# Layer 1 of a four-layer graph network: another order for the column numbers and the sums

## The chip, the cores and the metric

The kernel runs on one core of a Trainium2 chip. The metric is the device time of one execution in microseconds (us); the median of the runs is given. A core has five engines with a queue each: TensorE (PE in the profile; its weight loads, PEld, overlap with products), VectorE (DVE), ScalarE (ACT), GpSimd (POOL) and SyncE (SP), which here issues transfers. Each engine works through its own queue; engines meet at semaphores.

## The reference

Four layers of a graph network on 2708 nodes with 128 features and one weighted adjacency matrix, `adj`, in which well under one per cent of the entries are not zero. The change concerns layer 1 alone:

```python
def _L1_gnn_ref(node_feats, adj, msg_w, msg_b, upd_w, upd_b, ln_w, ln_b):
    s = node_feats @ msg_w[:, :D].T
    d = node_feats @ msg_w[:, D:].T
    messages = gelu(s[:, None, :] + d[None, :, :] + msg_b)
    aggregated = einsum('ijd,ij->id', messages, adj)
    combined = concatenate([node_feats, aggregated], axis=-1)
    new_feats = combined @ upd_w.T + upd_b
    h = gelu(new_feats) + node_feats
    # ... layer norm of h
# --- layer 1 ---
h = maximum(layernorm(x), 0.0)
x = x + _L1_gnn_ref(h, adj, ...)
```

A message is a gelu of a sum that belongs to a pair of nodes, so it can't be had from one product of matrices; but a message is only needed where `adj` has an entry. Layers 0, 2 and 3 (a plain sum over neighbours, a gated cell, attention) are not touched.

## The kernel before

Layer 0 reads `adj` once and lists, for each row and each block of 124 columns, up to 8 entries (`val`, `col`). Layer 1 works from these lists. Its rows come in 22 tiles of 128 (`NT = 22`) and its columns in 22 blocks (`NB = 22`, `HB = 11`). For each tile and block the entries are packed into up to 128 numbered slots; a 0/1 matrix `sel` says which row a slot belongs to, and a 0/1 matrix `cols` says which column. PE then makes the argument of the gelu of each slot as `sel * s + cols * d` (`s` and `d` split into three bf16 parts, hence three products each), ACT applies the gelu, and PE sums the messages of a row with a matrix `put`, which holds each entry's value in its row.

The steps for a tile, in the order in which they come (cuts are marked):

```python
def rank(t):          # first slot of each row: a product on PE, copies on DVE
    p = rpool.tile([P, CH], F32, tag="r", name="p_r")
    nc.tensor.matmul(p[:, 0:NB], before, rows_n[:, t, :], start=True, stop=True)
    nc.vector.tensor_copy(ends[:, t, :], p[:, 0:NB])
    ...
# describe(t): packs val and col into xb (ACT, DVE "v_r", POOL)
def select_rows(t):   # DVE, then a transfer that shifts sel by one row
    sel = selpool.tile([P, NB, E], BF16, name="sel")
    compare(sel, ends4, ALU.is_ge)
    nc.sync.dma_start(later[0:112, :, :], sel[1:113, :, :])
    ...
def finish_rows(t):   # DVE
    nc.vector.tensor_tensor(sel, sel, later, ALU.subtract)
def fetch(t, half):   # PE brings each slot its row's entries; ACT copies "lead"
    ...
    nc.tensor.matmul(y[:, b, :], st["sel"][:, bb, :], xb[t % 2][:, bb, :], start=True, stop=True)
    ...
def place(t):         # DVE: each slot's column number, value and row
    # ... slot, hot, picked
    nc.vector.tensor_reduce(where, picked[:, :, 3, :], AX.X, ALU.max)
    nc.vector.reduce_sum(value, picked[:, :, 0:3, :], AX.XY)
    mine = once.tile([P, NB, P], BF16, name="mine")
    compare(mine, lead[:, :, 0:R], ALU.is_equal)
def put_values(t):    # POOL: put = mine * value for blocks 0 to 10
    ...
def put_more(t, k):   # ACT: the same for blocks 11 to 21, some in each step
    for b in range(HB + 2 * k, min(HB + 2 * k + 2, NB)):
        nc.scalar.activation(st["put", 1][:, b - HB, :], st["mine"][:, b, :], AF.Identity, scale=st["value"][:, b : b + 1])
def pass_on(t):       # the column numbers are turned on PE and spread to all partitions
    p = rpool.tile([P, 2 * CH], BF16, tag="r", name="p_w")
    nc.tensor.transpose(p[0:NB, 0:E], st.pop("where"), ident_h)
    turned = work.tile([NB, E], BF16, name="where_T")
    nc.scalar.copy(turned, p[0:NB, 0:E])
    passed = wdram.tile([NB, E], BF16, name="passed")
    nc.sync.dma_start(passed, turned)
    st["spread"] = work.tile([P, NB, E], BF16, name="spread")
    nc.sync.dma_start(st["spread"]..., passed....partition_broadcast(P))
def columns(t):       # DVE
    nc.vector.tensor_scalar(st["cols"], st.pop("spread"), part, None, ALU.is_equal)
def sources(k):       # s of two tiles: PE "p_s", DVE "sb" and "s_r", ACT, POOL
    ...
def combine(t, k):    # PE: 4 blocks, each three products with sel and three with cols, into p_m
    ...
def activate(t, k):   # ACT: g = gelu(p_m)
    ...
def gather(t, k):     # PE: agg += g * put, one f32 product for each of 4 blocks (2 in the last
                      # group); the trace counts each f32 product as two
    ...
```

The pool `rpool` has one PSUM buffer, which `p_r`, `p_w`, `p_s` and the updates' `p_u` use in turn. `once` has one buffer per name, `work` two; `g` has three buffers and `p_m` two.

Five tiles are under way at a time. A period combines tile t and prepares those behind it, in six steps (`GB = 6`); the order in the program is the order in each engine's queue:

```python
for k in range(GB):
    if now:
        combine(t, k)
        activate(t, k)
    if k == 0:
        if last:
            gather(t - 1, GB - 1)
            close_tile(t - 1)
        if a:
            rank(t + 3)
    elif now:
        gather(t, k - 1)
    if k in (1, 2) and b:
        fetch(t + 2, k - 1)
    if k == 1 and a:
        describe(t + 3)
    if k == 2:
        if now and t % 2 == 0 and t + 2 < NT:
            sources(t // 2 + 1)
        if a:
            select_rows(t + 3)
        if now and t + 4 < NT:
            count_rows(t + 4)
        updates(t)
    if k == 3 and c:
        columns(t + 1)
    if c:
        put_more(t + 1, k)
    if k == 3 and b:
        place(t + 2)
    if k == 4 and b:
        pass_on(t + 2)
    if k == 4 and a:
        finish_rows(t + 3)
```

Here `now`, `c`, `b` and `a` say that tiles t, t + 1, t + 2 and t + 3 exist, and `last` that t - 1 does. `put_values(t + 1)` stands ahead of the steps. `updates` brings groups of four finished tiles through the layer's update, two small parts per period. Periods -3 to -1 are laid between the steps that end layer 0.

Of the kernel before, what the change touches and what calls it, by code (L numbers as in the profile page):

```python
# [21 lines left out]
BF16 = mybir.dt.bfloat16  # L22
# [8 lines left out]
P = 128  # L31
# [13 lines left out]
NB = (N + JB - 1) // JB  # L45
S = 8
E = P
# [4 lines left out]
def size(t):  # L52
    return min(P, N - t * P)
# [7 lines left out]
def listed_layers(ctx: ExitStack, tc: tile.TileContext, x, adj, w, out, flag):  # L61
# [111 lines left out]
    with tc.tile_pool(name="l0c", bufs=1) as fix:  # L173
# [4 lines left out]
        with (  # L178
# [6 lines left out]
            for gi, (g0, gk) in enumerate(GROUPS):  # L185
# [4 lines left out]
                for q in range(gk):  # L190
                    n = g0 + q
                    m = size(n)
                    a = a4[:, q, :]
# [26 lines left out]
                for j in range(NT):  # L220
                    k = size(j)
# [55 lines left out]
    HB = NB // 2  # L277
    R = 4
    C = 4 * S + R + 1
    with (  # L280
# [55 lines left out]
        def compare(dst, numbers, op):  # L336

            nc.vector.tensor_tensor(  # L338
                dst.rearrange("p b (x r) -> p b x r", r=R),
                count_h.rearrange("p (x r) -> p x r", r=R).unsqueeze(1).to_broadcast([P, NB, P // R, R]),  # L340
                numbers.unsqueeze(2).to_broadcast([P, NB, P // R, R]),
                op,
            )

        def rank(t):
# [3 lines that stand above are left out]
            nc.vector.tensor_copy(ends4, p[:, 0:NB].unsqueeze(2).to_broadcast([P, NB, R]))  # L349
# [35 lines left out]
        def place(t):  # L385

            st = state[t]
            lead = st["lead"]
            slot = work.tile([P, NB], F32, name="slot")
            nc.vector.tensor_scalar(slot, lead[:, :, R], part, -1.0, ALU.subtract, ALU.mult)  # L390
            hot = once.tile([P, NB, S], F32, name="hot")
            nc.vector.tensor_tensor(
                hot,
                count[:, 0:S].unsqueeze(1).to_broadcast([P, NB, S]),
                slot.unsqueeze(2).to_broadcast([P, NB, S]),
                ALU.is_equal,
            )
            picked = once.tile([P, NB, 4, S], F32, name="picked")
            for half, y in enumerate(st.pop("ys")):
                bs = slice(half * HB, (half + 1) * HB)  # L400
                nc.vector.tensor_tensor(
                    picked[:, bs, :, :],
                    y[:, :, 0 : 4 * S].rearrange("p b (q s) -> p b q s", s=S),
                    hot[:, bs, :].unsqueeze(2).to_broadcast([P, HB, 4, S]),
                    ALU.mult,
                )
            value = work.tile([P, NB], F32, name="value")
            where = work.tile([P, NB], BF16, name="where")
            with nc.allow_low_precision("column numbers"):
                nc.vector.tensor_reduce(where, picked[:, :, 3, :], AX.X, ALU.max)  # L410
            nc.vector.reduce_sum(value, picked[:, :, 0:3, :], AX.XY)
            mine = once.tile([P, NB, P], BF16, name="mine")
            compare(mine, lead[:, :, 0:R], ALU.is_equal)
            st["value"], st["where"], st["mine"] = value, where, mine

        def put_values(t):

            st = state[t]
            for half in range(2):
                st["put", half] = putpool.tile([P, HB, P], F32, name="put")  # L420
            nc.gpsimd.tensor_tensor(  # L421
                st["put", 0],
                st["mine"][:, 0:HB, :],
                st["value"][:, 0:HB].unsqueeze(2).to_broadcast([P, HB, P]),
                ALU.mult,
            )

        def put_more(t, k):

            st = state[t]  # L430
            for b in range(HB + 2 * k, min(HB + 2 * k + 2, NB)):
                nc.scalar.activation(  # L432
                    st["put", 1][:, b - HB, :], st["mine"][:, b, :], AF.Identity, scale=st["value"][:, b : b + 1]
                )

        def pass_on(t):

            st = state[t]
# [3 lines that stand above are left out]
            nc.scalar.copy(turned, p[0:NB, 0:E])  # L442
            passed = wdram.tile([NB, E], BF16, name="passed")
            nc.sync.dma_start(passed, turned)
            st["spread"] = work.tile([P, NB, E], BF16, name="spread")
            nc.sync.dma_start(
                st["spread"].rearrange("p b e -> p (b e)"), passed.rearrange("b e -> (b e)").partition_broadcast(P)
            )

        def columns(t):  # L450

            st = state[t]
            st["cols"] = work.tile([P, NB, E], BF16, name="cols")
            nc.vector.tensor_scalar(st["cols"], st.pop("spread"), part, None, ALU.is_equal)
# [35 lines left out]
        def combine(t, k):  # L490

            st = state[t]
            s3 = own_rows[t // 2][0]
            b0 = 4 * k
            n = min(4, NB - b0)
            p = mpool.tile([P, 4, D], F32, name="p_m")
            for b in range(b0, b0 + n):
                kb = width(b)
                for q in range(3):
                    nc.tensor.matmul(  # L500
                        p[:, b - b0, :], st["sel"][:, b, :], s3[:, q, t % 2, :], start=(q == 0), stop=False
                    )
                for q in range(3):
                    nc.tensor.matmul(  # L504
                        p[:, b - b0, :], st["cols"][0:kb, b, :], d3[0:kb, b, q, :], start=False, stop=(q == 2)
                    )
            st["p", k] = p

        def activate(t, k):
            n = min(4, NB - 4 * k)  # L510
            g = three.tile([P, 4, D], F32, name="g1")
            nc.scalar.activation(g[:, 0:n, :], state[t].pop(("p", k))[:, 0:n, :], AF.Gelu)  # L512
            state[t]["g", k] = g

        def gather(t, k):

            st = state[t]
            m = size(t)
            if k == 0 and t % 4 == 0:
                aggs[t // 4] = acc.tile([P, 4, P], F32, name="agg1")  # L520
            agg = aggs[t // 4][:, t % 4, 0:m]
            g = st.pop(("g", k))
            for b in range(4 * k, min(4 * k + 4, NB)):
                put = st["put", b // HB][:, b % HB, 0:m]
                nc.tensor.matmul(agg, g[:, b - 4 * k, :], put, start=(b == 0), stop=False)  # L525
# [62 lines left out]
        def updates(t):  # L588

            for g, (first, k) in enumerate(GROUPS):  # L590
                step = t - (first + k + 1)
                if 0 <= step < STEPS:
                    update(g, step)

        GB = (NB + 3) // 4

        def period(t):

            now, c, b, a = (0 <= t + q < NT for q in range(4))
            last = 0 <= t - 1 < NT  # L600
            if c:
                put_values(t + 1)
            for k in range(GB):
                if now:
                    combine(t, k)
                    activate(t, k)
                if k == 0:
                    if last:
                        gather(t - 1, GB - 1)
                        close_tile(t - 1)  # L610
                    if a:
                        rank(t + 3)
                elif now:
                    gather(t, k - 1)
                if k in (1, 2) and b:
                    fetch(t + 2, k - 1)
                if k == 1 and a:
# [6 lines that stand above are left out]
                    if now and t + 4 < NT:  # L624
                        count_rows(t + 4)
                    updates(t)
                if k == 3 and c:
                    columns(t + 1)
                if c:
                    put_more(t + 1, k)  # L630
                if k == 3 and b:
                    place(t + 2)
                if k == 4 and b:
                    pass_on(t + 2)
                if k == 4 and a:
                    finish_rows(t + 3)

# [262 lines left out]
    with (  # L900
# [135 lines left out]
        last = RUNS[0]  # L1036
# [12 lines left out]
    with tc.tile_pool(name="l3w", bufs=5) as wpool, tc.manual_schedule():  # L1049
        for run, numbers in zip(RUNS[1:], ((2, 3, 4, 5, 0, 1), (2, 3, 4, 5, 0, 1), (2, 3))):  # L1050
# [5 lines left out]
            last = run  # L1056
# [466 lines left out]
```

## Time and profile before

| | us |
|---|---|
| time, median of 3 runs (1163.88 to 1165.95) | 1165.69 |
| span of the profiled execution | 1161.2 |
| PE busy in it | 981.1 |
| DVE busy | 848.1 |
| ACT busy | 487.0 |
| POOL busy | 333.8 |

PE has products in 84% of the span, but the layers have different limits, so layer 1 has to be looked at by itself: its periods lie between 311 and 696 us. L500 and L504 are the products of `combine`, L525 those of `gather`, L440 the turn of the column numbers, L347 and L468 the products of `rank` and `sources`. On DVE, L338 is `compare` (for `sel` and for `mine`), L369 `finish_rows`, L454 `columns`, L410 and L411 `where` and `value`. On ACT, L512 is the gelu and L432 `put_more`; on POOL, L421 is `put_values`. In a line of waits, `A <- B: us, times, longest` means that A stood still until B was done. Columns of a timeline are start, length in us, engine, line, operation, output and inputs, shapes, count, and in brackets the idle time before it with what ended it.

### The profile page before, as it was taken

The numbers are of one execution on the slowest core, as the hardware profiler recorded it, in microseconds if no ns is written. First come the engines' busy times: TensorE is split into PE (matmuls) and PEld (weight loads), VectorE is DVE, ScalarE is ACT, GpSimd is POOL, SyncE is SP. The second block draws the span as 40 slices with busy tenths as digits, with TensorE's granted clock in tenths as the row PEclk, the third lists the DMA queues.
The fourth block names the chain that finished last, engine by engine and source line by source line (L and its number), as shares of the span: only waits on it lengthen the run. The fifth ranks groups of instructions, "written<-read, shape, count | busy, mean of one in ns | idle before, by whom it ended". The sixth has DMA issues, their size and how long they took to land. (4 is left out here: it accounts for less than half of the span.)

```text
span 1161.2 us, 21750 instructions
## 1 busy us (share of the span) xinstructions
PE 981.1 (84%) x7968; PEld 778.4 (67%) x7968; DVE 848.1 (73%) x2948; ACT 487.0 (42%) x1253; POOL 333.8 (29%) x312
## 2 busy tenths in 40 slices
PE   4987987803599998978889897999988999999993
PEld 1554544503488888978789893444457999999872
DVE  5999999988466656676666836565557887897683
ACT  4855656604455555546455452243333110140142
POOL 3111112013324433535334226343331020150042
PEclk9999889655599999989899897999999999999996
DMA  9587787411123222222212106554520000000000
GB/s 363 192 287 266 284 292 249 165 54 55 46 76 101 101 77 79 74 95 82 76 61 92 51 28 236 192 185 164 181 56 1 1 8 1 1 15 6 1 14 13
DMA packets 55297, 125.38 MB, mean 108 GB/s; under 512 B 7414, under 2 KB 19782, under 8 KB 52472
## 3 DMA queue, kind: packets, MB, share of 16 engines
q1 hardware_dynamic: 48590, 121.12, 30.0%
q10 hardware_dynamic: 6590, 2.77, 1.0%
q8 instruction: 64, 1.05, 0.4%
q14 instruction: 53, 0.43, 0.1%
HBM read 77.30 MB, written 30.84 MB: 93 GB/s over the span
## 5 line engine op out<-in xcount | busy, mean ns | idle before, releaser
L804 PE MATMUL att<-hv,wt 128*128 128x129 f32 (+2 forms) x1936 | 242.4, 282 | 9.2 <-DVE wt L772 9.2
L804 PEld LDWEIGHTS att<-hv,wt 128*128 128x128 f32 (+2 forms) x1936 | 223.4, 191 | 26.3 <-DVE wt L772 8.9
L772 DVE SCALAR_TENSOR_TENSOR wt<-row,lift,mask 128x1024 f32<-128x1024 f32 (+5 forms) x176 | 160.0, 939 | 34.0 <-PE att L804 34.0
L500 PE MATMUL p_m<-s,sel 128*128 128x128 bf16 x1452 | 168.4, 226 | 3.0 <-ACT s L323 1.9
L504 PE MATMUL p_m<-d,cols 124*128 124x128 bf16 (+1 forms) x1452 | 168.4, 226 | 0.0
L525 PE MATMUL agg<-put,g 128*128 128x128 f32 (+1 forms) x968 | 144.3, 293 | 10.9 <-ACT g L512 10.9
L196 PE MATMUL acc<-a,hs 128*128 128x512 f32 (+2 forms) x264 | 123.9, 606 | 25.8 <-DMA a<-in_adj 19.0
L525 PEld LDWEIGHTS agg<-put,g 128*128 128x128 f32 x968 | 126.0, 202 | 12.6 <-ACT g L512 12.6
L119 POOL TENSOR_TENSOR n_r<-n_r,minus_half 128x4 f32<-128x4 f32 (+1 forms) x36 | 48.2, 1340 | 295.5 <-DVE n_r L118 281.4
L217 DVE FIND_INDEX8 col<-val,a 128x8 uint16<-128x124 f32 (+1 forms) x441 | 119.9, 286 | 0.0
L512 ACT ACTIVATE g<-p_m 128x512 f32<-128x512 f32 x132 | 73.2, 555 | 110.1 <-PE p_m L504 109.2
L421 POOL TENSOR_TENSOR put<-mine,value 128x1408 f32<-128x1408 bf16 x22 | 79.8, 3629 | 132.7 <-DVE mine L338 125.6
L925 PE MATMUL p_agg<-a,hs 128*128 128x512 f32 (+2 forms) x264 | 110.4, 560 | 7.7 <-DVE n1u_st L116 4.4
L500 PEld LDWEIGHTS <-sel 128*128 128x128 bf16 x1452 | 107.9, 101 | 7.7 <-issue 3.6
L504 PEld LDWEIGHTS <-cols 124*128 124x128 bf16 (+1 forms) x1452 | 107.8, 101 | 0.6 <-issue 0.6
L216 DVE MAX8 val<-a 128x8 f32<-128x124 f32 (+1 forms) x441 | 103.7, 277 | 0.0
L196 PEld LDWEIGHTS acc<-a,hs 128*128 128x128 f32 (+1 forms) x264 | 50.2, 210 | 72.0 <-issue 43.9
L225 PEld LDWEIGHTS p_T<-ident,a 128*128 128x128 f32 x484 | 58.5, 145 | 53.6 <-ACT aT L229 25.6
L225 PE MATMUL p_T<-ident,a 128*128 128x128 f32 x484 | 77.2, 292 | 19.2 <-DMA a<-in_adj 10.0
L229 ACT ACTIVATE aT<-p_T 128x512 f32<-128x512 f32 (+2 forms) x132 | 71.0, 541 | 44.0 <-issue 19.6
L925 PEld LDWEIGHTS p_agg<-a,hs 128*128 128x128 f32 (+1 forms) x264 | 48.3, 195 | 56.0 <-issue 55.0
L432 ACT ACTIVATE put<-mine,value 128x128 f32<-128x128 bf16 x242 | 83.6, 391 | 0.0
(228 smaller groups left out, 1415.7 us busy)
## 6 DMA issues: line engine op xcount, KB each, us to landing
a<-in_adj SPq DMA_DIRECT2D x21, 1354.0 KB
adjT<-aT SPq DMA_DIRECT2D x105, 256.0 KB
a<-adjT SPq DMA_DIRECT2D x20, 1280.0 KB
spread<-passed SPq DMA_DIRECT2D x22, 704.0 KB
later<-sel SPq DMA_DIRECT2D x22, 616.0 KB
later<-sel SPq DMA_DIRECT2D x22, 82.5 KB
adjT<-aT SPq DMA_DIRECT2D x21, 74.0 KB
a<-adjT SPq DMA_DIRECT2D x4, 370.0 KB
```

The costliest lines, as they stand in the source:

```text
L196: nc.tensor.matmul(accs[ci][:, 0:cw], h[0:m, n, :], a[0:m, c : c + cw], start=(n == 0), stop=(n == NT - 1))
L216: nc.vector.max(val[:, n, b, :], ab)
L217: nc.vector.max_index(col[:, n, b, :], val[:, n, b, :], ab)
L225: nc.tensor.transpose(p[0:k, q * P : q * P + m], a4[0:m, q, j * P : j * P + k], ident[0:m, 0:m])
L421: nc.gpsimd.tensor_tensor(st["put", 0], st["mine"][:, 0:HB, :], st["value"][:, 0:HB].unsqueeze(2).to_broadcast([P, HB, P]), ALU.mult,)
L432: nc.scalar.activation(st["put", 1][:, b - HB, :], st["mine"][:, b, :], AF.Identity, scale=st["value"][:, b : b + 1])
L500: nc.tensor.matmul(p[:, b - b0, :], st["sel"][:, b, :], s3[:, q, t % 2, :], start=(q == 0), stop=False)
L504: nc.tensor.matmul(p[:, b - b0, :], st["cols"][0:kb, b, :], d3[0:kb, b, q, :], start=False, stop=(q == 2))
L525: nc.tensor.matmul(agg, g[:, b - 4 * k, :], put, start=(b == 0), stop=False)
L772: nc.vector.scalar_tensor_tensor(wt[0:kj, :], row[0:kj, k, c : c + n], lift[0:kj, j, k : k + 1], mask[0:kj, j, c : c + n], op0=ALU.max, op ...
L804: nc.tensor.matmul(banks[s // 3][0:m, s % 3, :], wt[0:kj, q * P : q * P + m], hv[0:kj, j, k, :], start=(v < 2 and s // 3 not in touched), ...
L925: nc.tensor.matmul(pa[:, 0:n], h[0:k, j, :], a[0:k, j - j0, 0:n], start=(j == 0), stop=(j == NT - 1))
```

## The change

Three things. The turn of the column numbers (`pass_on`) goes from step 4 of the period in which they are found to step 0 of the next one, so that PE need not wait for them; `columns` moves with it, from step 3 (ahead of `place`) to step 4 (behind it). The sums (`gather`) come two groups behind the messages instead of one, so that the gelu has more time; the last two groups of a tile are summed in the next period. And `mine` gets two buffers, so that it can be written while `put_more` still reads the last one, while `spread` needs only one. `put_more` does its eleven blocks in steps 1 to 5 (2, 2, 2, 2, 3) instead of 0 to 5.

```diff
--- before.py
+++ after.py
@@ -409,7 +409,7 @@
             with nc.allow_low_precision("column numbers"):
                 nc.vector.tensor_reduce(where, picked[:, :, 3, :], AX.X, ALU.max)
             nc.vector.reduce_sum(value, picked[:, :, 0:3, :], AX.XY)
-            mine = once.tile([P, NB, P], BF16, name="mine")
+            mine = work.tile([P, NB, P], BF16, name="mine")
             compare(mine, lead[:, :, 0:R], ALU.is_equal)
             st["value"], st["where"], st["mine"] = value, where, mine
 
@@ -428,7 +428,7 @@
         def put_more(t, k):
 
             st = state[t]
-            for b in range(HB + 2 * k, min(HB + 2 * k + 2, NB)):
+            for b in range(HB + (NB - HB) * (k - 1) // (GB - 1), HB + (NB - HB) * k // (GB - 1)):
                 nc.scalar.activation(
                     st["put", 1][:, b - HB, :], st["mine"][:, b, :], AF.Identity, scale=st["value"][:, b : b + 1]
                 )
@@ -442,7 +442,7 @@
             nc.scalar.copy(turned, p[0:NB, 0:E])
             passed = wdram.tile([NB, E], BF16, name="passed")
             nc.sync.dma_start(passed, turned)
-            st["spread"] = work.tile([P, NB, E], BF16, name="spread")
+            st["spread"] = once.tile([P, NB, E], BF16, name="spread")
             nc.sync.dma_start(
                 st["spread"].rearrange("p b e -> p (b e)"), passed.rearrange("b e -> (b e)").partition_broadcast(P)
             )
@@ -604,14 +604,17 @@
                 if now:
                     combine(t, k)
                     activate(t, k)
-                if k == 0:
+                if k < 2:
                     if last:
-                        gather(t - 1, GB - 1)
+                        gather(t - 1, GB - 2 + k)
+                    if k == 0 and c:
+                        pass_on(t + 1)
+                    if k == 0 and a:
+                        rank(t + 3)
+                    if k == 1 and last:
                         close_tile(t - 1)
-                    if a:
-                        rank(t + 3)
                 elif now:
-                    gather(t, k - 1)
+                    gather(t, k - 2)
                 if k in (1, 2) and b:
                     fetch(t + 2, k - 1)
                 if k == 1 and a:
@@ -624,14 +627,12 @@
                     if now and t + 4 < NT:
                         count_rows(t + 4)
                     updates(t)
-                if k == 3 and c:
-                    columns(t + 1)
-                if c:
+                if k > 0 and c:
                     put_more(t + 1, k)
                 if k == 3 and b:
                     place(t + 2)
-                if k == 4 and b:
-                    pass_on(t + 2)
+                if k == 4 and c:
+                    columns(t + 1)
                 if k == 4 and a:
                     finish_rows(t + 3)
```

## The prediction

> **What bounds the kernel now.** I read the table of stretches first, to find the stage the change touches. Layer 1's periods run from 311 to 696 us. Columns: stretch, length, busy time of PE, PEld, DVE, ACT, POOL with counts, granted clock, DMA share, GB/s.
>
> ```profile
> 311.00:696.00 385.00, 343.60 (x4520) 331.70 (x4518) 239.43 (x453) 199.72 (x558) 145.14 (x106) 0.93 0.22 75
> ```
>
> TensorE (PE) is busy 89% of the stage at a mean clock of 0.93: about 41 us idle, and a further loss because part of the work ran slower. VectorE (DVE) is at 62%, so no second engine is full on average. The waits between 320 and 680 us say who stops whom (us in total, times, longest):
>
> ```profile
> ACT g L512 <- PE p_m L504: 100.0, 85, 3.8
> ...
> DVE mine L338 <- ACT put L432: 32.8, 20, 2.3
> ...
> PE p_w L440 <- DVE where L410: 27.5, 16, 3.6
> ...
> PE agg L525 <- ACT g L512: 10.9, 10, 2.1
> ```
>
> PE has two waits only: turning the column numbers waits for `where` (27.5 us, in 16 of 20 periods), and the sums wait for the gelu before them (10.9 us). The change aims at both, and its second `mine` buffer at the 32.8 us of DVE. What such a wait does next is in PE's timeline (start, us, engine, line, operands, count, idle before):
>
> ```profile
> 457.60 1.16 PE L525 MATMUL agg<-put,g 128*128 128x128 f32 x8 [0.57 <-ACT g L512]
> 461.21 0.28 PE L440 MATMUL p_w<-ident_h,where 128*22 128x128 bf16 x1 [2.45 <-DVE where L410]
> 461.43 0.50 PE L500 MATMUL p_m<-s,sel 128*128 128x128 bf16 x3
> ...
> 467.83 0.33 PE L500 MATMUL p_m<-s,sel 128*128 128x128 bf16 x3
> ```
>
> After the 2.45 us wait three products take 0.50 to 0.53 us instead of 0.33, until 467.83: starts of three-product groups are 0.32 us apart instead of 0.17, so half speed. Over the stage such stretches add up to 34.5 us, about 17 us lost.
>
> DVE's timeline of the same period shows why `where` is late:
>
> ```profile
> 453.42 0.69 DVE L475 TENSOR_TENSOR sb<-p_s,msg_b 128x512 f32<-128x512 f32 x1 [2.56 <-PE p_s L468]
> ...
> 458.33 0.95 DVE L454 TENSOR_SCALAR cols<-spread,part 128x2816 bf16<-128x2816 bf16 x1
> 459.19 0.23 DVE L390 TENSOR_SCALAR slot<-lead,part 128x22 f32<-128x22 bf16 x1
> ...
> 460.82 0.34 DVE L410 TENSOR_REDUCE where<-picked 128x22 bf16<-128x176 f32 x1
> 461.08 0.69 DVE L411 TENSOR_REDUCE value<-picked 128x22 f32<-128x528 f32 x1
> 463.70 1.63 DVE L338 TENSOR_TENSOR mine<-count_h,lead 128x2816 bf16<-128x2816 bf16 x1 [1.93 <-ACT put L432]
> ```
>
> DVE idles 2.56 us for PE's products `p_s` of step 2 and then works without a break to `where`. So the period is a loop of two legs: PE from the turn at 443.22 to `sb` at 453.42 (10.20 us), DVE from `sb` to the end of `where` at 461.16 (7.74), a hand-over of 0.05; the sum is the 17.99 us between turns. In periods without source rows the DVE leg starts at `v_r` instead, which waits for ScalarE (ACT) and so for PE's step 1.
>
> **What the Trainium skill says.** "TensorE: Matmul & The Clock Gate", section "Architectural detail", says DVE and ACT are strict FIFO. The trace agrees: DVE sits 1.93 us at `mine` while `sel` behind it is ready. Its section "What's actually happening" says the clock is either full or half, set by windows of 3413 ns. The trace agrees on half, and waits of 2.4 us and more are mostly followed by 3 to 6.6 us of it; a wait of 1.57 us at 443.22 was not. "SBUF — State Buffer", section "Who interferes with whom", says that a `tensor_scalar` in a two-port mode and a GpSimd (POOL) operation exclude each other, the later one standing still. The trace agrees once: `cols`, usually 0.95 us, took 3.23 while POOL's `put` ran from 288.02 to 291.11.
>
> ```profile
> 288.63 3.23 DVE L454 TENSOR_SCALAR cols<-spread,part 128x2816 bf16<-128x2816 bf16 x1
> ```
>
> **The change, part by part.** *The turn* goes from step 4 of one period to step 0 of the next, so PE no longer waits for `where`: 27.5 us of waits go. But `columns` moves on DVE from before `place` to after it, and the next period's fourth product needs `cols`. One wait of PE on DVE is exchanged for another. I recompute the loop for the period above, now from `cols` to `cols`.
>
> PE leg, was 10.20. It starts later in PE's order: the turn (0.16), the last combine (0.64), one sum of eight (0.89) and three products that need no columns (0.16) leave it, 1.85 in all. It gains the turn at step 0 (0.13) and a new wait. `p_w` and `p_r` share one PSUM buffer and now follow each other directly, so `p_r` waits for ACT's copy: before, the turn began at 443.22 and the copy (0.25) at 443.48, so its end plus a hand-over is about 0.6 after the turn's start, 0.45 of it wait. The three sums inside the leg are the same sizes in another order. 10.20 - 1.85 + 0.58 = 8.93.
>
> DVE leg, was 7.74. `cols` only changes place (0). Behind `where` come the rest of `value` (461.16 to 461.77, 0.61) and `mine` (about 1.55; with two buffers it starts at once). 7.74 + 2.16 = 9.90.
>
> Sum with the hand-over: 18.9 against 17.99, or +0.9; I take +1.0. DVE's leg grows by more than PE's shrinks, and the same two differences hold in every period that this loop binds: 16 of 20, so +16 us. Four periods were bound by PE itself (13.74 us at the start of the stage); they gain the 0.45 of `p_r`, together +2.
>
> *Sums two groups behind:* the 10.9 us go, but those waits stand after `p_s` and before the hand-over, where PE has time to spare. Worth nearly 0 while DVE is last.
>
> *Second buffer for `mine`:* the 32.8 us stood behind `where`, and DVE afterwards idled at `v_r` or `sb` anyway. Worth 0 by itself, but it lets `mine` start at once where `cols` now waits behind it.
>
> *Half speed:* PE's idle time is 38.4 us now (27.5 + 10.9), in two pieces per period. With +1.0 per period and 0.45 more of known wait it becomes about 38.4 + 16 x 0.55 = 47 us, nearly in one piece, some 2.9 us each and over 5 in the longest. I judge that about five more periods start at half speed, each losing half of a window, 1.7 us: +8.
>
> *Before the stage:* the turn that held PE 12.36 us until 294.20 goes, but DVE was busy throughout. It saves `mine`'s 0.42 us of wait and the about 2.1 us that `cols` stood behind POOL: -2.5.
>
> *Transfer:* `spread` was issued at 445.02 and the DMA engines were quiet again from 448.3, 3.3 us later. Issued at about 4.5 us into the period it lands at 8, well before `cols` at 15 or later: 0.
>
> Sum: 16 + 2 + 8 - 2.5 = +23.5; 1165.7 + 23.5 = 1189, rounded up to 1190 for the second rival.
>
> **The rivals.** (1) *The waits simply go.* If DVE had `cols` in time, up to 38 us of idle and most of 17 us of half speed would vanish: about 1115. For it: PE's waits are the named ones, and DVE is only 62% busy. Against: the gaps of DVE lie at `v_r` and `sb`, early in the period, where it waits for PE; behind them there is none, and two operations are added ahead of the hand-over.
> (2) *POOL takes the shared port.* `mine` now releases `put` on POOL at the moment when `cols` starts. Now `put` starts 0.14 us after `mine` ends (446.73 to 446.87) and DVE's next instruction 0.09 before it, so DVE should come first. If POOL wins, `cols` stands still up to 2.5 us in each bound period: 16 x 2.5 = 40 more, about 1230. I give it one in five.
> (3) *Half speed doesn't grow.* Then +15: about 1181. The clock's windows run freely, so this is likely in part.
>
> **Range and chances.** The centre is the sum; the lower end (1168) is the loop at half its growth with no change of the clock and the early gain; the upper end (1225) is rival 2 nearly whole. Two per cent above 1165.7 is 1189, at my centre, so slower and same share nearly all: slower 0.50, same 0.45. Rival 1 gets 0.05.
>
> **What would show it.** Right: PE's wait on `where` is gone and one on `cols` (L454), of 40 us or more, stands in its place; a wait of about 0.45 us per period of `p_r` on ACT; PE's wait on `g` and DVE's on `put` nearly gone; the stage at 400 us or more; the clock below 0.93. Wrong: no wait on `cols`, or a stage under 375 us, would mean that DVE's order isn't the limit. `cols` at 3 us would show rival 2.

## The result, and the profile after

| | before | changed kernel |
|---|---|---|
| time, median (us) | 1164.79 | 1175.73 |
| lowest to highest | 1161.28 to 1165.95 | 1173.84 to 1178.98 |
| profiled span | 1161.2 | 1173.1 |

The ratio is 1.0102, with a 95% interval of 1.0069 to 1.0135: the change costs about 11 us, 1%. The stage is where it is lost. From the first product of period 0 to the last sum of tile 21, by the table of stretches (stretch, length, busy time of PE, PEld, DVE, ACT, POOL with counts, clock, DMA share, GB/s), before and then after:

```profile
313.00:695.10 382.10, 342.53 (x4515) 331.05 (x4514) 238.46 (x451) 198.28 (x553) 144.72 (x105) 0.94 0.22 75
```

```profile
313.30:705.80 392.50, 340.08 (x4516) 328.02 (x4515) 275.82 (x452) 197.15 (x554) 127.18 (x105) 0.95 0.22 75
```

Layer 1 is 10.4 us longer with the same work on PE, and the mean clock is not lower but a little higher. PE's waits between 320 and 690 us of the changed kernel:

```profile
PE p_m L504 <- DVE cols L454: 41.7, 14, 4.9
PE p_r L347 <- ACT where_T L442: 6.2, 18, 0.3
PE p_m L500 <- ACT g L512: 2.3, 2, 1.2
```

The wait for `where` (27.5 us) is gone and the one for the gelu fell from 10.9 to 2.3, but one on `cols` of 41.7 us has come, and 0.34 us per period on the shared PSUM buffer: 50.2 us of waits for 38.4. DVE's timeline of the period that was shown of the kernel before:

```profile
466.72 0.34 DVE L410 TENSOR_REDUCE where<-picked 128x22 bf16<-128x176 f32 x1
466.97 0.69 DVE L411 TENSOR_REDUCE value<-picked 128x22 f32<-128x528 f32 x1
467.58 1.62 DVE L338 TENSOR_TENSOR mine<-count_h,lead 128x2816 bf16<-128x2816 bf16 x1
469.12 0.95 DVE L454 TENSOR_SCALAR cols<-spread,part 128x2816 bf16<-128x2816 bf16 x1
469.98 3.96 DVE L369 TENSOR_TENSOR sel<-sel,later 128x2816 bf16<-128x2816 bf16 x1
```

and PE's timeline beside it:

```profile
466.20 0.33 PE L500 MATMUL p_m<-s,sel 128*128 128x128 bf16 x3
470.12 0.34 PE L504 MATMUL p_m<-d,cols 124*128 124x128 bf16 x3 [3.59 <-DVE cols L454]
```

`mine` starts at once now, as it was meant to, and `cols` comes behind it. PE does the three products that need no columns at 466.20 and stands for 3.59 us until `cols` is done. From one hand-over to the next (451.27 to 470.12) this period takes 18.85 us; the two legs were worked out as 18.9.

### The profile page after: what moved, and what is told of

It reads as the page before. It is cut to its first block, busy times and chain, and to the rows that moved or that the text cites. A ratio compares the mean times of both kernels' runs of the same rounds, so it can differ in the third digit from the quotient of the medians.

```text
span 1173.1 us, 21693 instructions
## 1 busy us (share of the span) xinstructions
PE 979.0 (83%) x7968; PEld 777.2 (66%) x7968; DVE 885.5 (75%) x2948; ACT 485.5 (41%) x1253; POOL 314.5 (27%) x312
## 5 line engine op out<-in xcount | busy, mean ns | idle before, releaser
L504 PE MATMUL p_m<-d,cols 124*128 124x128 bf16 (+1 forms) x1452 | 166.9, 225 | 41.7 <-DVE cols L454 41.7
L196 PE MATMUL acc<-a,hs 128*128 128x512 f32 (+2 forms) x264 | 121.1, 593 | 26.7 <-DMA a<-in_adj 19.9
L421 POOL TENSOR_TENSOR put<-mine,value 128x1408 f32<-128x1408 bf16 x22 | 67.3, 3058 | 84.1 <-DVE mine L338 79.1
L369 DVE TENSOR_TENSOR sel<-sel,later 128x2816 bf16<-128x2816 bf16 x22 | 79.6, 3617 | 5.4 <-DMA later<-sel 5.3
```

The lines of the kernel that those rows point to most:

```text
L196: nc.tensor.matmul(accs[ci][:, 0:cw], h[0:m, n, :], a[0:m, c : c + cw], start=(n == 0), stop=(n == NT - 1))
L504: nc.tensor.matmul(p[:, b - b0, :], st["cols"][0:kb, b, :], d3[0:kb, b, q, :], start=False, stop=(q == 2))
```

## The experiments

**Columns ahead of `place` again.** The theory is that DVE's order makes the loss. Against the changed kernel:

```diff
+                if k == 3 and c:
+                    columns(t + 1)
                 if k == 3 and b:
                     place(t + 2)
-                if k == 4 and c:
-                    columns(t + 1)
```

> The changed kernel with columns put back to step 3, ahead of place; the turn, the sums and the buffers stay as changed. Theory (VectorE's order: cols behind value and mine is what TensorE waits for): cols is ready about 4 us before it is needed, the wait on cols (41.7 us) goes, and finish_rows behind mine becomes the last hand-over in the longest periods only: periods of about 15.3 us with source rows, 14.2 without, 16 to 17 in the longest, so 1120 to 1130 us. Rival (half speed, the shared PSUM buffer or the transfer of spread cost the time, not the order): 1165 us or more. If the transfer is late, a wait of cols on spread shows.

Measured: 1126.34 us, ratio to before 0.9669 [0.964, 0.9698]. PE's waits from 320 to 640 us:

```profile
PE p_r L347 <- ACT where_T L442: 6.2, 18, 0.3
PE y L379 <- DVE sel L369: 3.3, 6, 0.9
PE p_m L500 <- ACT g L512: 2.3, 2, 1.2
PE p_m L504 <- DVE cols L454: 2.2, 3, 0.9
```

The wait on `cols` fell from 41.7 to 2.2 us. The table of stretches gives for the stage:

```profile
313.90:656.80 342.90, 326.66 (x4516) 316.30 (x4515) 243.99 (x452) 196.21 (x554) 145.14 (x105) 0.99 0.25 86
```

With almost no waits, the clock is not at half again after 323.1 us. The position of one 0.95 us instruction in DVE's queue is worth 49 us, and the rival falls. Part of the 49 us, about 13 by the filled kernels below, is half speed that goes together with the waits.

**Columns between `value` and `mine`:** a smaller dose of the same.

```diff
-        def place(t):
+        def place(t, between=None):
...
             nc.vector.reduce_sum(value, picked[:, :, 0:3, :], AX.XY)
+            if between is not None:
+                columns(between)
             mine = work.tile([P, NB, P], BF16, name="mine")
...
                 if k == 3 and b:
-                    place(t + 2)
-                if k == 4 and c:
+                    place(t + 2, t + 1 if c else None)
+                elif k == 3 and c:
                     columns(t + 1)
```

> The changed kernel with columns between value and mine, a smaller dose of the same: VectorE's leg to cols is shorter by mine alone, 1.55 us. Theory (order): 14 waits shorter by about 1.5 us each, so 18 to 22 us less than the changed kernel, about 1155. Rival (the order is not the limit): within 3 us of the changed kernel.

Measured: 1149.35 us, 0.9867 [0.9838, 0.9897], 26 us less than the changed kernel, where 18 to 22 were expected. The wait on `cols` is 20.7 us in 13 waits, 21.0 less, which is the 14 x 1.5 expected. The other 5 us fit less half speed: by the trace's record of the granted clock it was at half for 27.7 us of this stage, against 42.1 in the changed kernel.

**Rank one step later:**

```diff
-                    if k == 0 and a:
-                        rank(t + 3)
...
+                if k == 1 and a:
+                    rank(t + 3)
                 if k in (1, 2) and b:
                     fetch(t + 2, k - 1)
```

> The changed kernel with rank moved from step 0 to step 1, so that its product no longer follows the turn directly in the one PSUM buffer. Theory: the 0.34 us waits of p_r on ScalarE's copy lie on TensorE's leg in every period and go: 19 x 0.34 = 6 us less, about 1169. Rival (the waits are hidden behind VectorE's leg): 0 to 2 us less.

Measured: 1169.52 us, 1.0057 [1.0033, 1.008]; the wait of `p_r` is gone, and the medians are 6 us apart while the wait on `cols` is unchanged (41.7 us). It lies on PE's leg; with some 5 us of noise in that difference, the runs can't say whether all 6 us come off.

**PE's waits filled with extra products,** in the changed kernel and in the kernel before. Nothing else is moved; the extra products are overwritten or never read. `FILL` gives their number for each period.

```diff
             p = mpool.tile([P, 4, D], F32, name="p_m")
+            for i in range(FILL.get(t, 0) if k == 0 else 0):
+                nc.tensor.matmul(p[:, 0, :], st["sel"][:, 0, :], s3[:, 0, t % 2, :], start=True, stop=True)
```

> The changed kernel with extra products at the head of the periods that wait for cols: they write a part of p_m that the first real product overwrites, 14 to 70 of them per period, chosen to take 0.8 of the wait measured there. Nothing else moves. It shows what half speed costs: the slow stretches of the changed kernel add up to 28 us, so at most 14 us lost. If these lie on TensorE's leg of the loop: 9 to 14 us less, about 1163. If they are hidden: 0 to 3 us less.

In the kernel before the same loop stands in `pass_on`, ahead of the turn, and writes a tile of the pool `rpool`.

> The kernel before with extra products ahead of the turn, in the periods that wait for where, 9 to 51 of them, 0.8 of the wait measured there; they write a tile that nothing reads. Its slow stretches add up to 34.5 us, at most 17 us lost. If half speed costs the kernel before more than the changed kernel, the gain here is larger than in the changed kernel with its waits filled: 10 to 15 us less than before, about 1152, and the distance between the two filled kernels is near the 12 us by which TensorE's idle time grew. If half speed costs nothing: 1165.

Measured: the changed kernel filled 1162.62 us (0.9988 [0.9974, 1.0001]), the kernel before filled 1150.53 us (0.9883 [0.9861, 0.9904]): 13 and 14 us less than without the filling, for work that adds nothing. The table of stretches, first of the kernel before filled, then of the changed kernel filled:

```profile
313.00:681.40 368.40, 348.29 (x4888) 337.38 (x4887) 238.93 (x451) 199.09 (x554) 144.87 (x106) 0.99 0.23 78
```

```profile
313.30:692.00 378.70, 359.43 (x5102) 348.42 (x5101) 275.32 (x451) 196.91 (x554) 127.25 (x105) 0.99 0.23 78
```

Both reach a clock of 0.99. These two stretches begin at the times used above, but in these runs the first product of period 0 came at 314.30 and at 312.65. From it to the end of the last sum the stage shrinks from 381.9 to 366.9 us in the kernel before and from 392.3 to 379.1 in the changed one. The filled kernels are 12.2 us apart, the unfilled ones 10.4: the change's whole loss is there at full clock, and half speed has no part in it. In these profiles it cost the kernel before about 2 us more than the changed one; the medians (13.6 and 13.1 us less) don't resolve that.

Nearly without half speed, the periods can be compared one by one. These are the times between successive turns in the two filled kernels, in us, matched so that each column has the same steps 1 and 2 in it:

```
period     1     2     3     4     5     6     7     8     9    10
before 13.74 17.14 13.74 17.14 15.62 17.14 15.39 18.00 16.06 19.66
after  14.14 17.99 14.15 17.99 16.01 17.99 16.24 18.86 16.01 20.51
period    11    12    13    14    15    16    17    18
before 16.26 19.46 16.05 19.66 16.27 18.01 17.10 19.29
after  17.11 18.86 16.01 20.51 17.12 18.85 17.24 20.15
```

Eleven periods grew by 0.84 to 0.86 us each. Periods 1, 3 and 5 grew by about 0.4, and 9, 12, 13 and 17 by -0.6 to +0.14. Periods 12 and 17 belong with the eleven: what is left of half speed in the filled kernel before made them long there. In 12 its 13 extra products took 1.59 us, so that the turn came at 531.47 although `where` was done at 529.96; in 17 the products behind the turn were slow, so that `v_r` came 7.96 us after it instead of the 7.24 of the other periods. Without these 1.46 and 0.72 us both grew by about 0.85 (an estimate). So thirteen periods grew by 0.85; only 9 and 13 did not grow.

**The parts one by one, on the kernel before.** Sums two groups behind alone (with `put_more` in steps 1 to 5):

```diff
+                if k < 2:
+                    if last:
+                        gather(t - 1, GB - 2 + k)
+                    if k == 1 and last:
+                        close_tile(t - 1)
                 elif now:
-                    gather(t, k - 1)
+                    gather(t, k - 2)
```

> The kernel before with the sums two groups behind (and put_more in steps 1 to 5) alone. Theory: the 10.9 us of waits for the gelu go, but TensorE only waits the longer for where: within 3 us of before. Rival (those waits cost what they measure): 8 to 11 us less, about 1155. A part may come from fewer slow stretches: up to 5 us less.

Measured: 1166.79 us, 1.0032 [1.0019, 1.0045]. One wait is left in PE's list, and it holds the others' time:

```profile
PE p_w L440 <- DVE where L410: 41.3, 16, 4.9
```

The 10.9 us for the gelu are gone, and the wait for `where` rose from 27.5 to 41.3: PE arrived earlier and waited longer. The hoped-for few slow stretches less did not come: behind the start of period 0 the clock fell to half twelve times instead of eight.

Two buffers for `mine` alone (and one for `spread`):

```diff
-            mine = once.tile([P, NB, P], BF16, name="mine")
+            mine = work.tile([P, NB, P], BF16, name="mine")
```

> The kernel before with two buffers for mine and one for spread alone. Theory: VectorE's 32.8 us of waits for put_more stand where it waits for TensorE next anyway: within 2 us of before. Rival: up to 10 us less.

Measured: 1165.26 us, 1.0006 [0.9993, 1.0018]. The two waits of PE are the same as before to a tenth of a microsecond. DVE's own 32.8 us at `mine` went to the waits that follow: at `v_r` from 44.9 to 54.0, and at `ends`, for `p_r`, from 3.5 to 22.9.

The turn alone (`pass_on` in step 0 of the next period, `columns` behind `place`; one buffer for `mine`, sums one group behind):

> The kernel before with the turn moved to step 0 of the next period and columns behind place alone; mine keeps one buffer, the sums stay one group behind. Theory: this part alone makes the loss: and mine now also waits for ScalarE's last put_more (about 1.3 to 2 us) ahead of cols, so at least as slow as the changed kernel: 1176 to 1195. Rival (the loss comes from the sums or from buffers): near 1165.

Measured: 1211.93 us, 1.0406 [1.0379, 1.0433], 47 us more than before and above the range that was put (1176 to 1195). DVE's timeline of one of its periods:

```profile
507.21 1.62 DVE L338 TENSOR_TENSOR mine<-count_h,lead 128x2816 bf16<-128x2816 bf16 x1 [2.51 <-ACT put L432]
508.76 0.94 DVE L454 TENSOR_SCALAR cols<-spread,part 128x2816 bf16<-128x2816 bf16 x1
```

The wait of `mine` for ACT's last `put_more`, which cost nothing in the old order, now stands ahead of `cols`. All twenty hand-overs wait (51.0 us), the gelu's 10.9 us stay, and the clock was at half for 78.5 us of the stage instead of 48.3.

The turn and `mine`'s second buffer, without the sums, is the same kernel with the two lines of buffers of the change:

> The kernel before with the turn moved, columns behind place, and two buffers for mine; the sums stay one group behind. It splits the 36 us between the turn alone (1212) and the changed kernel (1176). If mine's wait for put_more, now ahead of cols, made the turn alone that slow: near the changed kernel, 1173 to 1183. If it was the sums one group behind (work that TensorE did ahead of the wait or in it): 1195 or more.

Measured: 1176.54 us, 1.0121 [1.0089, 1.0153], no different from the whole change. The second buffer mends 35 us of the damage that the turn with its columns did; the sums add nothing while DVE is last.

**The turn with columns ahead of `place`,** and nothing else of the change (`pass_on` in step 0; `put_more` now stands ahead of `columns` in the program, but they are in the queues of different engines):

```diff
+                    if c:
+                        pass_on(t + 1)
...
-                if k == 4 and b:
-                    pass_on(t + 2)
```

> The kernel before with the turn moved to step 0 of the next period and columns left ahead of place; mine keeps one buffer and the sums stay one group behind. It shows what the turn alone is worth with VectorE's old order, and what sums and buffers add there (the same with both ran in 1126). TensorE's waits on where and on cols go, those on the gelu (10.9 us) stay and now count, and mine waits for put_more ahead of finish_rows: 1132 to 1145. If sums and buffers are needed for it: 1155 or more.

Measured: 1135.24 us, 0.9755 [0.9731, 0.9779]. PE's list has the gelu's 10.9 us and no wait on `where` or `cols`. With sums and buffers the same order ran in 1126.34. So the two parts are worth about 9 us here, where PE is last, and were worth nothing where it wasn't.

**The best of these:** columns ahead of `place`, and rank in step 1.

> Columns ahead of place (1126 us alone) and rank one step later (6 us less in the changed kernel), together. TensorE is now what bounds most periods, so the 0.34 us waits of p_r still lie on its path: 6 us less than with columns ahead alone, about 1120. If rank's later copies on VectorE push select_rows and finish_rows back, the waits of fetch on sel (3.3 us now) grow and eat it: 1126.

Measured: 1118.24 us, 0.961 [0.9587, 0.9634], 46 us faster than the kernel before. PE's longest waits from 320 to 640 us are `fetch` for `sel` (5.3 us), the gelu (2.3) and `cols` (2.2).

## Why the direction was right and the size was not

The chain of reasons held, but for two periods. The turn's wait was exchanged for one on `cols`, the shared PSUM buffer costs its wait in every period (0.34 us, predicted 0.45), sums and buffer bring nothing behind DVE, and PE never waits for the transfer of `spread`. POOL did not take the port from `cols`, which always took 0.95 us. Period by period the loop grew by 0.85 us where 0.9 had been worked out. But the sum said +23.5 us, and +10.9 was measured. Two of the signs named did not come: the stage grew by 10.4 us and not by 15 (385 to 400), and the clock did not fall. The terms of the sum, with what the runs show:

| term of the sum | predicted | measured |
|---|---|---|
| periods bound by the loop | 16 x 1.0 = +16 | 13 x 0.85 = +11 |
| other periods | +2 | 3 x 0.4, and 0 in two: +1 |
| half speed | +8 | about -2 (10.4 - 12.2) |
| ahead of the stage | -2.5 | +0.3 |

The step that failed most is half speed: "I judge that about five more periods start at half speed, each losing half of a window, 1.7 us: +8." It had no source in a trace; it was a guess from longer waits to more half speed. The waits did become longer and whole, as foreseen, yet from 320 us on the clock fell to half eight times in both kernels, and its time at half in the stage went from 48.3 to 42.1 us.

The traces show why. In each of them the granted clock changes only at the ends of windows of 3.41 us, and what it does next goes with how long PE had no product within one window. The table of stretches of the changed kernel, cut at these windows, around its wait on `cols` of 2.73 us that ended at 367.57 and the one of 2.72 that ended at 401.03 (PE's busy time stands behind the length, the clock third from the end):

```profile
365.63:369.04 3.41, 1.47 (x23) 1.47 (x24) 3.33 (x3) 0.01 (x1) 2.22 (x1) 1.00 0.00 0
369.04:372.45 3.41, 3.07 (x24) 2.76 (x23) 2.60 (x3) 0.84 (x2) 0.87 (x1) 0.50 0.01 2
...
396.35:399.76 3.41, 1.96 (x25) 1.76 (x22) 3.34 (x6) 2.54 (x9) 0.00 (x0) 1.00 0.62 202
399.76:403.18 3.42, 2.15 (x29) 2.12 (x29) 3.42 (x3) 0.60 (x1) 2.90 (x1) 1.00 0.00 0
403.18:406.59 3.41, 3.07 (x52) 2.93 (x51) 1.92 (x3) 1.03 (x4) 0.19 (x1) 1.00 0.16 40
```

The first wait left PE without products for 1.94 us of one window, and the next ran at half speed. The second wait was cut at 399.76 into 1.45 and 1.27 us, and the clock stayed full. In layer 1 of all thirteen profiles, from 320 us on, 1281 windows ran at full clock. The 79 of them that were followed by half speed had 1.80 us or more without products, the other 1202 had 1.87 or less. So a wait of 2.4 to 2.8 us costs half speed or not by where a window ends. And joining two short waits need not cost more: in the kernel before, the waits of 1.09 us for the gelu and 1.07 for `where` (to 426.40) fell almost wholly into one window, 1.91 us of it, and half speed followed there too. This is read from the traces; no run moved a single wait against the windows.

The second is the count: "the same two differences hold in every period that this loop binds: 16 of 20". They held in thirteen. Of the other three, period 0 isn't in the list of times above, and in periods 9 and 13 DVE had a delay in the old order that the new one mostly avoids: `cols` and `slot` took longer while POOL worked on `u`, a part of the updates. In the kernel before, period 9:

```profile
475.01 1.27 POOL L580 TENSOR_TENSOR u<-u,ln_w 128x512 f32<-128x512 f32 x1 [1.04 <-ACT u L135]
...
475.66 1.36 DVE L454 TENSOR_SCALAR cols<-spread,part 128x2816 bf16<-128x2816 bf16 x1
...
476.35 1.79 POOL L580 TENSOR_TENSOR u<-u,ln_b 128x512 f32<-128x512 f32 x1
...
476.94 1.24 DVE L390 TENSOR_SCALAR slot<-lead,part 128x22 f32<-128x22 bf16 x1
```

and in the changed kernel:

```profile
481.89 0.65 DVE L390 TENSOR_SCALAR slot<-lead,part 128x22 f32<-128x22 bf16 x1
...
486.33 0.95 DVE L454 TENSOR_SCALAR cols<-spread,part 128x2816 bf16<-128x2816 bf16 x1
```

The two took 2.60 us before and 1.60 after, and 1.18 in an undisturbed period. The 1.00 us won is more than the 0.85 lost, so `cols` is in time there, and PE's own work sets the period: 15.68 us (16.05 less its wait of 0.37 for `where`) and the 0.34 of `p_r`, which gives the 16.01 in the list. The prediction says that the trace shows POOL in the way of `cols` "once"; that was misread, for it took 1.36, 1.36 and 1.34 us in periods 9, 13 and 17 of the same trace. And 0.9 was rounded up to 1.0.

The third is small: ahead of the stage `cols` did leave POOL's way and took 0.95 us instead of 3.23, but `slot` moved into its place and stood there instead, 2.52 us against 0.51. `finish_rows` began 0.6 us earlier (296.10 instead of 296.72), yet the first product of period 0 came at 313.33 us instead of 313.02. That time moves from run to run by more: it was 312.65 in the changed kernel filled, whose program is the same up to there.

The first rival, that the waits simply go, came true not for this change but for the version that leaves `columns` ahead of `place`: 1126 us, where 1115 had been put.

## What to carry to other kernels

When a wait of the last engine is moved, ask which instruction of the other engine releases it afterwards, and count what stands ahead of that one in its queue: here two operations of 2.2 us in the hand-over's way cost the whole gain, and the same change with one line elsewhere gained 3.3%. A wait measured in the profile is worth its length only where nothing stands behind it: a second buffer for `mine` was worth 0, 35 us or a part of 9, depending on what its wait held up. To price half speed, fill the waits with products that nobody reads and look at the difference, rather than guess it; and see in the trace whether the filling itself made a period longer, as in period 12.

## What the runs showed of the hardware

Filling waits with useless products made both kernels faster by 13 to 14 us, for PE came out of its waits at full speed. From full clock, half speed followed every window of 3.41 us in which PE had no product for more than 1.87 us, and none with less than 1.80 (79 of 1281 windows, in thirteen profiles). And `finish_rows` on DVE (a `tensor_tensor` with both inputs in SBUF) took 3.57 to 3.96 us instead of 1.62 when POOL's `put` had started first; its mean in the changed kernel is 3.93 us over 19 of them. In this order it cost nothing: behind all but the last of them DVE idled 1.88 us or more at `v_r`. DVE's busy time went from 238.46 to 275.82 us in the stage for the most part by standing still.
